# Statistics of seven early layernorms split between VectorE and GpSimd, and a new planned order of all engines, in a four-layer graph network

## The chip, the cores and the metric

The kernel runs on one core of a Trainium2 chip. The metric is the device time of one execution in microseconds (us). A core has five engines with a queue each: TensorE (PE in the profile; its weight loads are PEld), VectorE (DVE), ScalarE (ACT), GpSimd (POOL) and SyncE (SP), which here only starts transfers (DMAs).

## The reference

x is 32 graphs of 512 nodes with 128 features, adj a 512 x 512 matrix of zeros and ones. Each of the four layers adds a network of a layernorm to x:

```python
def _layernorm(x, axis=-1, eps=1e-5):
    m = jnp.mean(x, axis=axis, keepdims=True)
    v = jnp.var(x, axis=axis, keepdims=True)
    return (x - m) / jnp.sqrt(v + eps)

h = jnp.maximum(_layernorm(x, axis=-1), 0.0)
x = x + _L0_gnn_ref(h, adj, ...)   # edge scores: sigmoid(a_tgt + a_src), times a mask of adj; two ELUs
h = jnp.maximum(_layernorm(x, axis=-1), 0.0)
x = x + _L1_gnn_ref(h, adj, adj, ...)   # five gated steps with adj @ h: gates z and r, candidate tanh
h = jnp.maximum(_layernorm(x, axis=-1), 0.0)
x = x + _L2_gnn_ref(h, adj, ...)   # adj @ (h @ weight) + bias
h = jnp.maximum(_layernorm(x, axis=-1), 0.0)
x = x + _L3_gnn_ref(h, adj, adj, ...)   # h, adj @ h, adj^2 @ h, adj^3 @ h, each times a weight, summed
```

## The kernel before, in words

The program first describes its work to a planner and then issues it in the order that the planner finds. Each `op(engine, us, due, emit, reads, writes, ...)` is one step: an engine, an assumed duration, a due time, a function that issues its instructions, and the values that it reads and writes. `Plan.order` plays the engines through with those assumed times: on each engine the ready step with the earliest due time goes first, and buffers are given out as they come free. The result is a fixed order for every engine; on the chip each engine works its own queue strictly in that order and waits by semaphores. `Plan.nudge` draws random shifts of due times, one draw for each seed in `HEAD_NUDGES` (steps due from 0 to 130) and `TAIL_NUDGES` (steps due after 1430; empty before), so a seed more or less changes the order everywhere after it. `plan.idle` (L375) is a product of ones on TensorE that the planner puts in, in the first 50 us, where TensorE would have nothing to do.

`A_LANDS` holds for each of the four quarters of the adjacency when the planner takes it to have landed after its DMA was issued; two are loaded from SyncE's queue, two from ScalarE's. `adjacency_turned` (L608) transposes the quarters on TensorE. VectorE counts the entries that are not zero or one (L594, summed on TensorE at L623), and the program then branches: the arm for a binary adjacency is the one that runs. In it the adjacency's square is made at L974 (products in fp32r, one pass), and the masks on GpSimd (L892).

A graph is 512 rows of 128 in four blocks of 128 rows (`NC` = 4). The graphs go through the layers staggered, up to five groups of four in flight. `layernorm` (L544) has these steps: on VectorE the statistics of each block (`bn_stats`, L553, four instructions: count, mean and squared deviations of the even and of the odd elements), their joining to mean and variance (`bn_aggr`, L555, four), and one addition of epsilon (L556); on GpSimd the power -1/2 (L558); then either, with ReLU, the shift on VectorE (L562) and four scalings on ScalarE (L567), or, for graphs 0 to 3 in layer 0, four normalisations on VectorE (L573), where the ReLU comes after a transpose. `entry` makes the layernorm of layer 0, `layer1`'s is made in the loop at the end of `list_rest`.

Layer 0: `scored` makes the first ELU (exponential, tanh and ReLU on ScalarE; L641, L646 and L648 on VectorE), the messages and scores (L711, L718), and `aggregated` the masked edge scores (L757 on ScalarE, L760 on VectorE), their products (L769), row sums (`totals`, on GpSimd's and SyncE's queues, L680 and L802), a second ELU and the output products (L830), which are added to x at L541. Layer 1: products with the adjacency in fp32r (L1018), with the gates' weights in fp32 (L521, two passes each), gates on VectorE and ScalarE (L1043 to L1064, L526), and transposes by blocks through DRAM (L462 on VectorE, then a DMA `m<-f` and one `f<-m`). Layer 3 has products with folded weights (L1093), with the squared adjacency (L1106), the last addition (L1125) and the stores.

Of the kernel before, what the change touches and what calls it, by code (L numbers as in the profile page):

```python
# [15 lines left out]
ALU = mybir.AluOpType  # L16
# [3 lines left out]
EPS = 1e-5  # L20
STEPS = 5


HEAD, TAIL = 250.0, 1430.0
HEAD_NUDGES = (7100008, 7100429, 7300015, 7100544, 7100583, 7300139, 7300091, 7300684, 7300016, 7300033, 7300035,
    7300041, 7300077, 7300137, 7300140, 7300167, 7300172, 7300174, 7300178, 7300506, 7300199,
    7300249, 7300263, 7300279, 7300298, 7300305, 7300507, 14000074, 14000497, 7300344, 7300346,
    7300367, 7300389, 7300391, 7300393, 7300406, 7300423, 14000795, 7300482, 7300509, 7300510,
    7300530, 7300532, 7300539, 7300544, 14000157, 7300549, 7300551, 7300553, 7300562, 7300570,
    14000024, 14000577, 7300614, 7300629, 7300644, 14000027, 14000360, 7300654, 7300663, 7300681,  # L30
    14000347, 7300696, 14000026, 14000010, 14000014, 14000195, 14000023, 14000035, 14000039,
    14000042, 14000045, 14000046, 14000048, 14000088, 14000208, 14000563, 14000122, 14000125,
    14000164, 14000166, 14000167, 14000181, 14000182, 14000252, 14000186, 14000187, 14000189,
    14000198, 14000204, 14000210, 14000212, 14000213, 14000739, 14000219, 14000227, 14000231,
    14000243, 14000275, 14000289, 14000299, 14000304, 14000306, 14000385, 14000319, 14000324,
    14000325, 14000326, 14000333, 14000338, 14000345, 14000346, 14000355, 14000358, 14000364,
    14000665, 14000398, 14000472, 14000417, 14000426, 14000427, 14000432, 14000438, 14000440,
    14000451, 14000458, 14000463, 14000469, 14000485, 14000486, 14000515, 14000520, 14000521,
    14000647, 14000528, 14000531, 14000540, 14000596, 14000560, 14000561, 14000815, 14000569,
    14000570, 14000580, 14000589, 14000591, 14000597, 14000602, 14000605, 14000606, 14000609,  # L40
    14000629, 14000638, 14000654, 14000661, 14000689, 14000678, 14000681, 14000685, 14000686,
    14000697, 14000698, 14000700, 14000703, 14000708, 14000715, 14000716, 14000721, 14000723,
    14000725, 14000726, 14000732, 14000734, 14000744, 14000751, 14000753, 14000755, 14000788,
    14000796, 14000801, 14000804, 14000807, 14000808, 14000811, 14000816, 14000817, 14000818,
    14000822, 14000827, 14000829, 14000831, 14000836, 14000839, 14000842, 14000843, 14000847,
    14000849, 14000850, 14000851, 14000852, 14000853, 14000855, 14000856, 14000857, 14000860,
    14000864, 14000870, 14000871)
TAIL_NUDGES = ()


class Val:
# [222 lines left out]
def tile_four_graph_layers(  # L274
# [27 lines left out]
    nc = tc.nc  # L302
    B, N, D = x.shape
    NC = N // P
    G = 4
# [4 lines left out]
    PACE, FIRST_PACE, LAST_PACE = 56.0, 10.0, 30.0  # L310
    BRANCH, FILL = 9.0, 50.0
    MARGIN = 10.0
    FIRST = 4
    FIRST_TREE, TREES, TREE = 4, 30, 52
    ONES, COPIES = 0, 32
    HALF = 2
    SQUARE, NAT = 11.0, 3.0
    BRANCHES = 0.75
    A_LANDS = (3.87, 3.05, 4.2, 4.0)

    T_MM, T_TR, T_NARROW, T_PASS = 0.86, 0.44, 0.224, 0.23
    T_VEC, T_COPY, T_ACT, T_DMA = 0.605, 0.5, 0.6, 0.45
# [3 lines left out]
    op = plan.op  # L326
# [22 lines left out]
    def at(v):  # L349
        if v.tile is not None:  # L350
            return v.tile
        return places[v.kind][v.slot] if v.whole is None else at(v.whole)[:, v.part]
# [15 lines left out]
    ident, ones, neg_half = const("ident", [P, P]), const("ones", [P, P]), const("nhalf", [P, NC])  # L368
# [31 lines left out]
    X = [Val(whole=X_group[b // G], part=b % G) for b in range(B)]  # L400
# [11 lines left out]
    A_nat = [Val("f") for _ in range(NC)]  # L412
# [128 lines left out]
            nc.vector.tensor_tensor(xv, xv, t, op=ALU.add)  # L541
        op("DVE", T_VEC, due, add, [X[b], p], [X[b]], two=two)

    def layernorm(b, due, relu=True, earliest=0.0):  # L544

        s, h = Val("s"), Val("f")
        def stat(lo, k=1):
            t = at(s)[:, lo * NC : (lo + k) * NC]
            return t if k == 1 else t.rearrange("p (c k) -> p c k", k=k)
        VAR, SCALE, SHIFT, PAIRS, STATS = 0, 1, 2, 4, 6  # L550
        def moments():
            for c in range(NC):
                nc.vector.bn_stats(stat(STATS, 6)[:, c, :], at(X[b])[:, c, :])  # L553
            for c in range(NC):
                nc.vector.bn_aggr(stat(PAIRS, 2)[:, c, :], stat(STATS, 6)[:, c, :])  # L555
            nc.vector.tensor_scalar(stat(VAR), stat(PAIRS, 2)[:, :, 1], EPS, None, op0=ALU.add)  # L556
        op("DVE", 1.26, due, moments, [X[b]], [s], earliest=earliest)
        op("POOL", 1.2, due, lambda: nc.gpsimd.tensor_tensor(  # L558
            stat(SCALE), stat(VAR), at(neg_half), op=ALU.pow), [s, neg_half], [s], two=False)
        mean = lambda: stat(PAIRS, 2)[:, :, 0]  # L560
        if relu:
            op("DVE", 0.1, due, lambda: nc.vector.scalar_tensor_tensor(  # L562
                stat(SHIFT), mean(), -1.0, stat(SCALE), op0=ALU.mult, op1=ALU.mult),
                [s], [s], two=True)
        def scale():
            for c in range(NC):
                nc.scalar.activation(  # L567
                    at(h)[:, ts(c, P)], at(X[b])[:, c, :], AF.Relu,
                    bias=stat(SHIFT)[:, c : c + 1], scale=stat(SCALE)[:, c : c + 1],
                )  # L570
        def normed():
            for c in range(NC):
                nc.vector.tensor_scalar(  # L573
                    at(h)[:, ts(c, P)], at(X[b])[:, c, :], mean()[:, c : c + 1],
                    stat(SCALE)[:, c : c + 1], op0=ALU.subtract, op1=ALU.mult)
        if relu:
            op("ACT", 1.56, due, scale, [X[b], s], [h])
        else:
            op("DVE", 1.03, due, normed, [X[b], s], [h])
        return h  # L580
# [11 lines left out]
    for ic in range(NC):  # L592
        odd = Val("f")
        op("DVE", 0.62, -1, lambda ic=ic, odd=odd: nc.vector.scalar_tensor_tensor(  # L594
            at(odd), at(A_nat[ic]), 0.0, at(A_nat[ic]),
            op0=ALU.is_gt, op1=ALU.not_equal, accum_out=at(n_odd[ic])),
            [A_nat[ic]], [odd, n_odd[ic]], two=True)
    def by_token(v):
        return at(v).rearrange("p (t c) -> p c t", c=NC)

    def adjacency_turned(due):
        banks = [Val("b") for _ in range(NC)]
        for pt in banks:
            pt.pieces = True
        for ic in range(NC):
            def turn(ic=ic):
                for jc, pt in enumerate(banks):
                    nc.tensor.transpose(at(pt)[:, ts(ic, P)], by_token(A_nat[ic])[:, jc, :], at(ident))  # L608
            op("PE", T_TR, due + ic, turn, [A_nat[ic], ident], banks)
        return banks  # L610

    adj_r = rows_of(const("adj_r", [P, NC, N], F32R).tile)
# [225 lines left out]
    def begin(b):  # L838
        steady = min(b, B - G - 1)
        return max((steady - G) * PACE + (b - steady) * LAST_PACE, b * FIRST_PACE)  # L840

    def entry(b):
        h = layernorm(b, begin(b), relu=b >= FIRST, earliest=begin(b) - 12.0 if b < G else 0.0)
        return first_turned(b, h, begin(b)) if b < G else turned_back(h, begin(b))

    begun = [scored(b, entry(b), begin(b)) for b in range(G)]
# [14 lines left out]
    def arm(binary):  # L861
        with ExitStack() as stack:
# [11 lines left out]
            if not binary:  # L874
                issue(plan.order())
                return
            plan.nudge(0.0, 130.0, HEAD_NUDGES)
            order = [*plan.order(end=HEAD), *plan.order(end=TAIL)]
            plan.nudge(TAIL, 2000.0, TAIL_NUDGES)
            issue(order + plan.order())  # L880

    def list_rest(binary, pool):
# [70 lines left out]
        for half in range(2):  # L953
            t, outs = Val("f"), slice(half * P // 2, (half + 1) * P // 2)
# [206 lines left out]
        for g in range(NG):  # L1161
            bs = range(g * G, (g + 1) * G)
            hT, uT = [], []
            for b in bs:
                if g:
                    load_graph(b, max(begin(b) - 40, 4 + b))
                    aggregated(b, scored(b, entry(b), begin(b)), begin(b), halves)
                t = begin(b) + (0.75 if b < G else 2.2 if b < B - G - 1 else 1.2) * PACE
                layer1(b, layernorm(b, t), t + 6, G * PACE / STEPS)
                t += (G + 0.5) * PACE  # L1170
                layer2(b, layernorm(b, t), t + 6)
                t += 0.5 * PACE
                h = layernorm(b, t)
                if g < NG - 1:
                    hT.append(turned_back(h, t + 4, in_order=True))
                else:
                    hT.append(copied(transposed(h, t + 6), t + 6))
                if binary:
                    uT.append(copied(times_adj(parts(h, t + 4, two=True), t + 6), t + 6))

            layer3(g, hT, uT, t + 12, {NG - 2: 16.0, NG - 1: 8.0}.get(g, 14.0))
            X_group[g].left -= 1
# [46 lines left out]
```

## Time and profile before

| what | before |
|---|---|
| median of 3 runs (range) | 1594.95 us (1594.51 to 1596.13) |
| profiled execution | 1594.3 us |
| its span | 1592.4 us |
| mean granted TensorE clock | 0.999 |
| busy VectorE, ScalarE, GpSimd | 1414.9, 1135.6, 303.8 us |
| `bn_aggr` (L555), 512 instructions | 46.6 us busy |
| addition of epsilon (L556), 128 instructions | 22.0 us busy |
| power on GpSimd (L558), 128 instructions | 156.0 us busy |

The times are those of the profiled execution from its span's start. "Busy" sums an engine's instructions. A group line gives line, engine, operation, output and input, shape and count, then busy us and mean ns, then the idle time of the engine ahead of it with what ended it. The chain of work that ended last is followed back from the last instruction, at each step to what released it, and is shown in order of time: start, us, what. A two-pass fp32 product stands as two records.

### The profile page before, as it was taken

What the parts mean: (1) busy time and instruction counts of PE and PEld (TensorE: products, weight loads), DVE (VectorE), ACT (ScalarE), POOL (GpSimd) and SP (SyncE); (2) the same over time, 40 slices, a digit from 0 to 9 for tenths busy, and PEclk for the clock granted to TensorE, in tenths of its full rate; (3) what the DMA queues carried; (4) which work ended last, traced back from release to release, by engine and by line L of the source; (5) the groups of instructions that cost most, each with busy time, mean ns of one, the idle gap of its engine ahead of it and who ended that gap; (6) DMA issues with size and microseconds to landing.
All of it is one profiled execution on the core that took longest, in us unless ns stands there. A gap on an engine that the chain in (4) does not pass through costs nothing.

```text
span 1592.4 us, 21245 instructions
## 1 busy us (share of the span) xinstructions
PE 1586.2 (100%) x6279; PEld 1017.0 (64%) x6279; DVE 1414.9 (89%) x3367; ACT 1135.6 (71%) x2151; POOL 303.8 (19%) x297
## 2 busy tenths in 40 slices
PE   9999999999999999999999999999999999999998
PEld 7655555666666666666666666666666666656688
DVE  8999999999988999898999989989899898988772
ACT  7877776877776777677876777667687676755661
POOL 3322112212211212211222121221221111000010
PEclk9999999999999999999999999999999999999999
DMA  4465545564554556554555545555556554322221
GB/s 129 94 164 145 157 120 133 127 170 120 138 144 122 141 145 146 132 139 126 147 146 142 143 116 148 128 139 137 139 152 151 129 140 125 96 86 87 93 54 56
DMA packets 303062, 204.92 MB, mean 129 GB/s; under 512 B 94936, under 2 KB 245080, under 8 KB 302936
## 3 DMA queue, kind: packets, MB, share of 16 engines
q1 hardware_dynamic: 260808, 175.63, 36.0%
q0 software_dynamic: 39984, 26.38, 13.1%
q10 hardware_dynamic: 2144, 1.44, 0.3%
q8 instruction: 52, 0.85, 0.2%
q14 instruction: 74, 0.61, 0.1%
HBM read 96.41 MB, written 103.68 MB: 126 GB/s over the span
## 4 chain that ended last, share of the span: by engine, by line
PE 95%; DVE 2%; DMA 2%; ACT 0%; issue 0%; SPq 0%; DVEq 0%
PE b L521 43%; PE b L1018 26%; PE b L1093 7%; PE b L769 6%; PE b L1106 4%; PE b L830 3%; PE b L1081 2%; PE b L711 2%; PE b L821 2%; DMA f<-m 0%; DVE f L760 0%; DMA m<-f 0%; DMA f<-in_adj_dram 0%; DMA f<-d 0%; DVE f L648 0%; DVE f L646 0%
## 5 line engine op out<-in xcount | busy, mean ns | idle before, releaser
L510 ACT COPY f<-b 128x512 f32<-128x512 f32 x414 | 238.5, 585 | 179.2 <-PE b L1018 121.5
L558 POOL TENSOR_TENSOR s<-s,nhalf 128x4 f32<-128x4 f32 x128 | 156.0, 1221 | 768.8 <-DVE s L556 745.6
L1043 DVE TENSOR_TENSOR f<-f,b 128x512 f32<-128x512 f32 x320 | 213.5, 680 | 49.6 <-PE b L521 43.3
L1018 PE MATMUL b<-AQ,r 128*128 128x512 f32 x848 | 256.4, 432 | 0.0
L567 ACT ACTIVATE f<-x,s 128x128 f32<-128x128 f32 x496 | 204.2, 488 | 20.7 <-DVE s L562 18.4
L462 DVE STREAM_TRANSPOSE f<-f 128x512 f32<-128x512 f32 x246 | 206.5, 846 | 7.6 <-ACT f L567 6.3
L1018 PEld LDWEIGHTS b<-AQ,r 128*128 128x128 f32 x848 | 158.9, 188 | 69.5 <-issue 31.4
L1018 PE MATMUL b<-adj_r,r 128*128 128x512 f32 x640 | 193.7, 428 | 0.0
L526 ACT ACTIVATE f<-f,b4w 128x512 f32<-128x512 f32 x160 | 115.3, 721 | 96.4 <-DVE f L1043 95.6
L521 PE MATMUL b<-f,w4T 128*128 128x512 f32 x320 | 163.2, 593 | 0.1
L521 PE MATMUL b<-f,u5T 128*128 128x512 f32 x320 | 163.1, 593 | 0.0
L521 PE MATMUL b<-f,w5T 128*128 128x512 f32 x320 | 162.9, 592 | 0.0
L521 PE MATMUL b<-f,w3T 128*128 128x512 f32 x320 | 162.8, 592 | 0.0
L521 PE MATMUL b<-f,u3T 128*128 128x512 f32 x320 | 161.7, 592 | 0.0
L1018 PEld LDWEIGHTS b<-adj_r,r 128*128 128x128 f32 x640 | 120.0, 188 | 50.0 <-issue 21.3
L526 ACT ACTIVATE f<-b,b5w 128x512 f32<-128x512 f32 x160 | 109.5, 686 | 50.3 <-PE b L521 49.5
L526 ACT ACTIVATE f<-f,b3w 128x512 f32<-128x512 f32 x160 | 114.8, 719 | 35.7 <-DVE f L1043 35.0
L680 POOL DMA_DIRECT2D m<-f x78 | 71.0, 910 | 333.1 <-DVE f L1060 45.3
L1093 PEld LDWEIGHTS b<-V,f 128*128 128x128 f32 x1024 | 122.2, 192 | 16.0 <-issue 13.9
L1060 DVE TENSOR_TENSOR f<-f,f 128x512 f32<-128x512 f32 x160 | 109.2, 683 | 24.3 <-ACT f L526 23.6
L988 ACT CAST r<-f 128x512 fp32r<-128x512 f32 x197 | 120.5, 617 | 12.6 <-DMA f<-m 9.6
L992 DVE TENSOR_TENSOR r<-f,r 128x512 fp32r<-128x512 f32 x168 | 113.9, 682 | 12.9 <-ACT r L988 12.8
(138 smaller groups left out, 2665.9 us busy)
## 6 DMA issues: line engine op xcount, KB each, us to landing
m<-f SPq DMA_DIRECT2D x272, 256.0 KB
f<-m SPq DMA_DIRECT2D x186, 256.0 KB
m<-f POOLq DMA_DIRECT2D x78, 256.0 KB, 4.2
f<-m SPq DMA_DIRECT2D x240, 64.0 KB
f<-d SPq DMA_DIRECT2D x54, 256.0 KB
x<-in_x_dram SPq DMA_DIRECT2D x32, 256.0 KB
out_dram<-x SPq DMA_DIRECT2D x28, 256.0 KB
d<-y SPq DMA_DIRECT2D x54, 64.0 KB
```

What stands on the lines that cost most here:

```text
L462: op("DVE", us, due, lambda: nc.vector.transpose(view_out(at(blocks)), view_in(at(src))), [src], [blocks])
L510: op("ACT", us, due, lambda: nc.scalar.copy(at(t), at(src)), [src], [t])
L521: nc.tensor.matmul(to, at(w), of, start=start, stop=stop)
L526: op("ACT", us, due, lambda: nc.scalar.activation(at(dst), at(src), AF.Tanh, bias=at(bias), scale=scale), [src, bias], [dst])
L558: op("POOL", 1.2, due, lambda: nc.gpsimd.tensor_tensor(stat(SCALE), stat(VAR), at(neg_half), op=ALU.pow), [s, neg_half], [s], two=False)
L567: nc.scalar.activation(at(h)[:, ts(c, P)], at(X[b])[:, c, :], AF.Relu, bias=stat(SHIFT)[:, c : c + 1], scale=stat(SCALE)[:, c : c + 1],)
L988: op("ACT", T_COPY, due, lambda: nc.scalar.copy(part(hi), whole()), [src], [hi], keep=1)
L992: op("DVE", T_VEC, due, lambda: nc.vector.tensor_tensor(part(lo), whole(), part(hi).bitcast(F32), op=ALU.subtract), [src, hi], [lo], two=two)
L1018: nc.tensor.matmul(at(pa), at(part)[:, ts(jc, P)], view(at(columns[jc])), start=jc == n == 0, stop=jc == NC - 1 and n == PARTS - 1,)
L1043: op("DVE", T_VEC, d, lambda: nc.vector.tensor_tensor(at(s), at(u), at(pg), op=ALU.add), [u, pg], [s])
L1060: op("DVE", T_VEC, d, lambda c=c, h=h: nc.vector.tensor_tensor(at(c), at(c), at(h), op=ALU.subtract), [c, h], [c], two=True)
L1093: nc.tensor.matmul(at(pz)[:, ts(i, D)], at(t[i])[:, ts(ic, P)], at(V[k]), start=i == graphs[0] and n == 0, stop=last and i == graphs[-1] a ...
```

## The change

1. `layernorm` gets a second form, `by_pool`, for graphs 1, 2, 3 in layer 0 and 0 to 3 in layer 1. VectorE makes only the `bn_stats`; GpSimd joins the halves itself with eight small instructions on 128 x 4 elements, and then takes the power as before.
2. `A_LANDS` has other assumed landings, and the transpose of an adjacency quarter is taken as 0.48 us instead of 0.44. Both are numbers for the planner alone.
3. `HEAD_NUDGES` is another, longer list of seeds, of which some are those of before, and `TAIL_NUDGES` has 24 seeds.

The second and third issue nothing themselves, but the order of every engine comes out of them.

```diff
-HEAD_NUDGES = (7100008, 7100429, 7300015, 7100544, 7100583, 7300139, 7300091, 7300684, 7300016, 7300033, 7300035,
...
-TAIL_NUDGES = ()
+HEAD_NUDGES = (7100008, 7100429, 7300139, 7300016, 7300033, 7300041, 7300137, 7300140, 7300167, 7300174, 7300178,
...
+TAIL_NUDGES = (40500041, 40500004, 40500007, 40500043, 40500032, 40500075, 40500021, 40500022, 40500023, 40500082,
...
+    POOL_0, POOL_1, POOLED = (1, 2, 3), (0, 1, 2, 3), 1.7
...
-    A_LANDS = (3.87, 3.05, 4.2, 4.0)
+    A_LANDS = (4.2, 3.05, 4.7, 4.28)
...
-    def layernorm(b, due, relu=True, earliest=0.0):
+    def layernorm(b, due, relu=True, earliest=0.0, by_pool=False):
...
+        if by_pool:
+            MEAN, T, U = 4, 5, 3
+            even, odd = (lambda k: stat(STATS, 6)[:, :, k]), (lambda k: stat(STATS, 6)[:, :, 3 + k])
+            def stats():
+                for c in range(NC):
+                    nc.vector.bn_stats(stat(STATS, 6)[:, c, :], at(X[b])[:, c, :])
+            op("DVE", 0.9, due, stats, [X[b]], [s], earliest=earliest)
+            def moments():
+                tt, ts1 = nc.gpsimd.tensor_tensor, nc.gpsimd.tensor_scalar
+                tt(stat(T), even(1), odd(1), op=ALU.subtract)
+                tt(stat(U), even(2), odd(2), op=ALU.add)
+                tt(stat(T), stat(T), stat(T), op=ALU.mult)
+                ts1(stat(T), stat(T), D / 4.0, None, op0=ALU.mult)
+                tt(stat(VAR), stat(T), stat(U), op=ALU.add)
+                ts1(stat(VAR), stat(VAR), 1.0 / D, EPS, op0=ALU.mult, op1=ALU.add)
+                tt(stat(MEAN), even(1), odd(1), op=ALU.add)
+                ts1(stat(MEAN), stat(MEAN), 0.5, None, op0=ALU.mult)
+                tt(stat(SCALE), stat(VAR), at(neg_half), op=ALU.pow)
+            op("POOL", 1.2 + POOLED, due, moments, [s, neg_half], [s], two=False)
+            mean = lambda: stat(MEAN)
+        else:
...
-            op("PE", T_TR, due + ic, turn, [A_nat[ic], ident], banks)
+            op("PE", 0.48, due + ic, turn, [A_nat[ic], ident], banks)
...
-        h = layernorm(b, begin(b), relu=b >= FIRST, earliest=begin(b) - 12.0 if b < G else 0.0)
+        h = layernorm(b, begin(b), relu=b >= FIRST, by_pool=b in POOL_0, earliest=begin(b) - 12.0 if b < G else 0.0)
...
-                layer1(b, layernorm(b, t), t + 6, G * PACE / STEPS)
+                layer1(b, layernorm(b, t, by_pool=b in POOL_1), t + 6, G * PACE / STEPS)
```

## The prediction

> **What bounds the kernel now.** I read four views in this order: the page's busy times, the groups of TensorE instructions by shape, the chain that ended last, and the waits of TensorE. The first:
>
> ```profile
> PE 1586.2 (100%) x6279; PEld 1017.0 (64%) x6279; DVE 1414.9 (89%) x3367; ACT 1135.6 (71%) x2151; POOL 303.8 (19%) x297
> ```
>
> A busy TensorE (PE) at 100% proves nothing by itself, since ends of matmuls are modelled. So I count the work by issue intervals. The chain gives them, where it stays on TensorE:
>
> ```profile
> 163.37 8.58 PE b L521 x20
> ...
> 279.91 3.71 PE b L1018 x16
> ...
> 1566.00 8.93 PE b L1093 x80
> ```
>
> That is 0.429 us for one record of a two-pass fp32 product 512 wide (8.58/20), 0.232 for an fp32r one 512 wide, 0.1116 for one 128 wide. The groups by shape give the counts, of which the largest and the idle products are:
>
> ```profile
> L1018 PE MATMUL b<-AQ,r 128*128 128x512 f32 x848 | 256.4, 432 | 0.0
> L521 PE MATMUL b<-f,w4T 128*128 128x512 f32 x320 | 163.2, 593 | 0.1
> L1093 PE MATMUL b<-V,f 128*128 128x128 f32 x1024 | 123.5, 275 | 0.0
> L375 PE MATMUL b<-ones 128*128 128x128 f32 x70 | 11.8, 320 | 1.0 <-DVE ones L370 1.0
> ```
>
> All groups together: 1992 records of fp32 512 wide (L521 1672, L769 256, L821 64) at 0.429 are 854.6 us; 2068 of fp32r 512 wide (L1018 1792, L1106 248, three small groups 28) at 0.232 are 479.8; 2125 of 128 wide without the idle ones at 0.1116 are 237.2; the rest 2.2. Sum: 1573.8 us. The first transpose starts at 6.13 us, the last matmul ends its issue at 1588.0: 1581.9 us. So only 8.1 us after the adjacency's arrival is not needed work. Of that, 50 of the 70 records of L375 (products of ones that the order puts in while TensorE has nothing) are 5.6, and true idle time about 2.5. Ahead stand 6.1 us (loads), behind 4.4 us (the last addition and its store). The whole profiled execution is 1594.3 us, 1.9 above its span and 0.65 below the median of 1594.95.
>
> So whatever the new order does, it can win at most 8.1 us (0.5%). The change takes no product of the computation away; it moves them.
>
> The chain shows where the little slack is made:
>
> ```profile
> 20.35 0.29 DVE s L555 x4
> 20.64 0.02 issue
> 20.66 0.17 DVE s L556
> ...
> 51.39 1.16 PE b L711 x8
> ```
>
> From 19.2 to 51.4 us it lies on VectorE (DVE), which is busy 39.8 of the 40 us from 20 to 60, and 0.48 us of it is L555 and L556 of each layernorm. After 51.4 it is on TensorE with short breaks.
>
> **The change part by part.** *The statistics.* Seven layernorms (graphs 1 to 3 in layer 0, 0 to 3 in layer 1) lose L555 and L556 on VectorE: 7 x 0.48 = 3.4 us off VectorE, about half of it inside the stretch where VectorE is the chain. GpSimd (POOL) gets eight small instructions more for each. Their nearest rows, and that of the power, which stays:
>
> ```profile
> 20.91 1.01 POOL L558 TENSOR_TENSOR s<-s,nhalf 128x4 f32<-128x4 f32 x1 [2.24 <-DVE s L556]
> ...
> 22.09 0.18 POOL L936 TENSOR_TENSOR b5w<-b5w,b5u 128x1 f32<-128x1 f32 x1
> 22.24 0.22 POOL L939 TENSOR_SCALAR b3w<-b3w 128x1 f32<-128x1 f32 x1
> ...
> 67.41 0.54 POOL L960 COPY V<-f 128x64 f32<-128x64 f32 x1
> ...
> 72.83 3.29 POOL L960 COPY V<-f 128x64 f32<-128x64 f32 x1
> ```
>
> Start to start the small ones are 0.2 us, so the chain is 8 x 0.2 + 1.0 = 2.6 us, against 1.0 now. The Trainium skill speaks against it: its page GPSIMD Engine Reference, Specifications, says that GpSimd's SBUF interfaces are shared with VectorE and contended by VectorE instructions with two SBUF inputs. L960 above agrees: 0.54 us once, 3.29 beside two-input instructions of VectorE (L1050, L760). If each small instruction had to let one of them (0.68 us) pass, the chain would be 8 x 0.88 + 1.4 = 8.4 us. But the power itself, on operands of the same 128x4, has a median of 1.32 and a maximum of 1.99 over 128 uses, most of them beside a busy VectorE: a stretch of 1.3. I take 2.6 x 1.3 = 3.4 us and keep 2.6 to 8.4. The planner allows 2.9.
>
> Who waits: on VectorE the shift (L562) or, in layer 0, the normalisation L573, and everything behind it. In the new order graph 1's L573 follows just one other statistics instruction, so VectorE will stand still there: its statistics end at about 10.9 us, the bias scaling and 2.6 to 3.4 us follow on GpSimd, so L573 begins near 14.0 to 14.7 and not at 13.2 as now. Behind it is graph 0's ELU (L646), which now starts at 15.1; L573 takes 1.1 us, so it is 0 to 0.7 us late. TensorE has all 16 products of the adjacency's square ahead of it in the new order, and idle products after them, so I charge 0 to 0.5 us. The masks (L892, 0.62 us each) come behind the chain, at about 14 to 17 instead of 10.8 to 14.8; they are first read at 23.3, so they are covered by 6 us, and would cost their own lateness without.
>
> *What VectorE's relief gives.* At the rows' durations, VectorE's work ahead of the first addition to x (L541) falls from 42.1 to 37.7 us in the new order, TensorE's up to the output products before it from 43.1 to 41.4; at the sixth addition it is 149.8 to 141.3 and 145.5 to 141.5. So VectorE is less behind than now, by some 3 to 4 us. But TensorE has little to gain from it: the order holds 32 idle products of ones instead of 35 (two records each). One more stands before the adjacency, where TensorE waits anyway until 6.13; 21 instead of 25 stand after it: 4 x 0.22 = 0.9 us. Two of these are in the wait for the count of odd entries, which VectorE sets, so they turn into idle time: 0.4 us remains sure, 0.9 at best.
>
> *Waits.* The trace's own:
>
> ```profile
> PE b L608 <- DMA f<-in_adj_dram: 0.5, 1, 0.5
> PE b L830 <- DVE f L648: 0.2, 1, 0.2
> ```
>
> By the starts of TensorE's instructions in the timeline, gaps of over 0.05 us after 8 us sum to 2.5 us, 2.0 of them before 150 us (the larger at 20.0, 51.4, 73.6, 125.2). With VectorE less behind, a third of the early ones should go (-0.7); the new order brings its own, as any order does whose times were assumed beforehand (+0.5, as much as the present one shows after 150).
>
> *The landings (A_LANDS), the transposes' 0.48, the nudges.* These are numbers for the planner alone and cost nothing themselves. The adjacency's transposes stand in the same order as now and wait for the same load; SyncE's first loads are the same twelve. TAIL_NUDGES move work after about 1430 us, where the gaps are a few hundredths of a us each, and the last products and stores are the same: 0. All other orders change too, with no work added.
>
> Sum: -0.6 - 0.7 + 0.5 + 0.2 = -0.6 us on the profiled 1594.3, so 1593.7, and with the 0.65 us to the median 1594.3.
>
> By another rule the sum would differ. The Trainium skill (Perfetto Trace Analysis, Identifying the Most-Contended Engine) calls matmul busy time a bad measure and takes weight loads' busy share instead. That is 64% here, which would leave 36% of the span free and make VectorE (89%) the engine to relieve; its 3.4 us would then show in full, 1591.5. The issue intervals above leave 8.1 us, so here the weight loads mislead, and I keep -0.6.
>
> **The rivals.** *A: VectorE's relief counts in full* and the order uses it: -3.4 us or more, 1588 to 1591.7. For it: the chain on VectorE from 19 to 51 us. Against: TensorE is idle or on idle products for only about 4 us there, and the new order still holds 15 idle products behind the branch (now 17). Chance 0.06.
>
> *B: GpSimd's chain is near its upper bound.* If it is over about 4 us, VectorE waits at the seven L562 and L573 for some 1 us each, at a time when it has no slack, and TensorE behind it: +4 us, 1598 to 1600, slower. For it: 3.29 us of L960. Against: the stretch of 1.3 of the power. Chance 0.07.
>
> *C: the new order meets a transfer later than assumed.* The blocks turned through DRAM land 3 to 7 us after their issue (6.60 us for one m<-f at 553, which ends in the gap at 568.5). Several such gaps of 0.5 to 2 us would give +2 to +6, 1596.5 to 1600. Against: after 150 us the present order loses 0.5 us in all. Chance 0.15, with 0.09 of it over the bound.
>
> The forecast (0.72) covers 1592.5 to 1597. That the change does nothing to the time lies in it.
>
> **How the numbers follow.** A measurement tells about 0.2% (3.2 us), so 1591.8 to 1598.1, from no change. Faster: A, 0.06. Slower: 0.07 + 0.09 = 0.16. Same: 0.78. The range from 1592.3 to 1598.0 leaves out A and the slower parts of B and C, about 0.2.
>
> **What would show it.** Right: some 64 records of L375's successor, gaps of TensorE of 2 to 3 us in sum, a VectorE chain that ends before 50 us, GpSimd's nine instructions in 2.6 to 3.7 us, and the same 4.4 us at the end. Wrong: idle gaps of TensorE of over 4 us in sum, each to be named by its releaser (GpSimd for B, a DMA for C), or a span under 1589 (A).

## The result and the profile after

The changed kernel takes 1600.12 us (median of 9 runs, 1599.11 to 1601.79) against 1594.95 before (also 9 runs): a ratio of 1.0033 with a 95% interval of 1.0025 to 1.0042, so 5.2 us slower. The profiled execution has a span of 1599.0 us, 6.6 more than before. The page's busy times after:

```profile
PE 1588.5 (99%) x6273; PEld 1016.4 (64%) x6273; DVE 1411.5 (88%) x3332; ACT 1140.0 (71%) x2151; POOL 324.7 (20%) x353
```

VectorE has 3.4 us less, as summed; GpSimd has 20.9 more. TensorE's work is the same, so the time must be in its gaps. Its waits after, the longest four of the change's stretch (who waited for whom: us, times, longest):

```profile
PE b L774 <- DVE f L711: 1.3, 1, 1.3
PE b L832 <- DVE f L823: 1.1, 1, 1.1
...
PE b L893 <- DVE f L711: 0.9, 1, 0.9
PE b L563 <- DMA f<-m: 0.5, 1, 0.5
```

(Line numbers of the changed kernel are 42 to 63 higher: L711 is L648 of before, L774 L711, L823 L760, L832 L769, L893 L830, L563 L521, L625 L562, L636 L573. L602 to L609 are the eight new instructions on GpSimd, L610 is the power.) The first gap's origin is seen in the timeline of GpSimd and VectorE (start, us, engine, line):

```profile
47.26 0.68 DVE L709 SCALAR_TENSOR_TENSOR f<-f,f 128x512 f32<-128x512 f32 x1
47.42 1.78 POOL L602 TENSOR_TENSOR s<-s 128x4 f32<-128x4 f32 x1 [16.66 <-DVE s L598]
47.85 0.68 DVE L858 TENSOR_TENSOR f<-f,f 128x512 f32<-128x512 f32 x1
48.45 0.69 DVE L711 SCALAR_TENSOR_TENSOR f<-f,f 128x512 f32<-128x512 f32 x1
49.06 0.22 DVE L781 TENSOR_SCALAR s<-b,be_quarter 128x4 f32<-128x4 f32 x1
49.16 1.98 POOL L603 TENSOR_TENSOR s<-s 128x4 f32<-128x4 f32 x1
49.19 0.68 DVE L858 TENSOR_TENSOR f<-f,f 128x512 f32<-128x512 f32 x1
49.79 0.69 DVE L709 SCALAR_TENSOR_TENSOR f<-f,f 128x512 f32<-128x512 f32 x1
50.39 0.68 DVE L858 TENSOR_TENSOR f<-f,f 128x512 f32<-128x512 f32 x1
51.09 0.19 POOL L604 TENSOR_TENSOR s<-s 128x4 f32<-128x4 f32 x1
...
52.62 1.05 POOL L610 TENSOR_TENSOR s<-s,nhalf 128x4 f32<-128x4 f32 x1
53.70 0.16 DVE L625 SCALAR_TENSOR_TENSOR s<-s 128x4 f32<-128x4 f32 x1 [2.63 <-POOL s L610]
53.78 0.68 DVE L711 SCALAR_TENSOR_TENSOR f<-f,f 128x512 f32<-128x512 f32 x1
```

L602 and L603 are instructions on 128 x 4 elements that take 0.2 us elsewhere. Here each ends only when a row of VectorE's instructions with two SBUF inputs ends: 47.26 to 49.14, then 49.19 to 51.07. Between the rows stands L781, which reads PSUM, and one small instruction gets through. Then VectorE comes to L625, which needs the chain, and stands still for 2.63 us; behind it waits L711, and behind that TensorE's L774, which starts at 54.61 after a gap of 1.3 to 1.5 us. The seven chains from L602 to the power's end take 2.90, 3.55, 5.24, 6.24, 5.30, 5.05 and 3.37 us (4.5 on average) where the planner had 2.9. VectorE's waits for the power, in the shift and in the normalisation:

```profile
DVE s L625 <- POOL s L610: 4.8, 4, 2.6
DVE f L636 <- POOL s L610: 4.4, 2, 2.9
```

The first of these six waits (2.94 us) stands behind the first chain, which ran without a hold in 2.90: it is the chain's length alone. The other five (1.42, 2.63, 1.57, 0.40 and 0.21 us) are each shorter than what their chain took over 2.90 (2.34, 3.34, 2.40, 2.15 and 0.47 us). By the timeline these chains would have been done in time without the holds. No kernel with the same eight instructions unheld was run, so this division into length and hold is read from the trace and not measured by itself.

### The profile page after: what moved, and what is told of

Same layout as the page of the kernel before. It is cut to its first block, busy times and chain, and to the rows that moved or that the text cites. A ratio compares the mean times of both kernels' runs of the same rounds, so it can differ in the third digit from the quotient of the medians.

```text
span 1599.0 us, 21231 instructions
## 1 busy us (share of the span) xinstructions
PE 1588.5 (99%) x6273; PEld 1016.4 (64%) x6273; DVE 1411.5 (88%) x3332; ACT 1140.0 (71%) x2151; POOL 324.7 (20%) x353
## 4 chain that ended last, share of the span: by engine, by line
PE 95%; POOL 2%; DVE 1%; DMA 1%; issue 1%; ACT 0%; SPq 0%; POOLq 0%
PE b L563 44%; PE b L1081 26%; PE b L1156 7%; PE b L832 6%; PE b L1169 4%; PE b L893 3%; PE b L1144 2%; PE b L884 2%; PE b L774 1%; DVE f L823 0%; DMA f<-d 0%; POOL s L610 0%; DMA d<-y 0%; DMA f<-in_adj_dram 0%; DMA bi_sb<-in_L_gnn_bi_dram 0%
## 5 line engine op out<-in xcount | busy, mean ns | idle before, releaser
L621 POOL TENSOR_TENSOR s<-s,nhalf 128x4 f32<-128x4 f32 x121 | 148.7, 1229 | 723.8 <-DVE s L619 656.5
L1081 PE MATMUL b<-AQ,r 128*128 128x512 f32 x856 | 260.5, 434 | 0.0
L1081 PE MATMUL b<-adj_r,r 128*128 128x512 f32 x616 | 188.5, 428 | 0.0
L563 PE MATMUL b<-f,w3T 128*128 128x512 f32 x320 | 162.9, 592 | 0.0
L563 PE MATMUL b<-f,w4T 128*128 128x512 f32 x320 | 162.9, 592 | 0.0
L563 PE MATMUL b<-f,w5T 128*128 128x512 f32 x320 | 162.6, 592 | 0.0
L563 PE MATMUL b<-f,u5T 128*128 128x512 f32 x320 | 162.4, 592 | 0.0
L563 PE MATMUL b<-f,u3T 128*128 128x512 f32 x320 | 161.4, 592 | 0.5 <-DMA f<-m 0.5
L1081 PEld LDWEIGHTS b<-adj_r,r 128*128 128x128 f32 x616 | 115.1, 188 | 45.9 <-issue 17.9
L1156 PE MATMUL b<-V,f 128*128 128x128 f32 x1024 | 123.7, 275 | 0.0
```

Of the source, the lines that this page charges most:

```text
L563: nc.tensor.matmul(to, at(w), of, start=start, stop=stop)
L621: op("POOL", 1.2, due, lambda: nc.gpsimd.tensor_tensor(stat(SCALE), stat(VAR), at(neg_half), op=ALU.pow), [s, neg_half], [s], two=False)
L1081: nc.tensor.matmul(at(pa), at(part)[:, ts(jc, P)], view(at(columns[jc])), start=jc == n == 0, stop=jc == NC - 1 and n == PARTS - 1,)
L1156: nc.tensor.matmul(at(pz)[:, ts(i, D)], at(t[i])[:, ts(ic, P)], at(V[k]), start=i == graphs[0] and n == 0, stop=last and i == graphs[-1] a ...
```

## The experiments

Two theories stood at the start. Theory 1: GpSimd's chain is held up and keeps VectorE's queue, and TensorE, waiting. Theory 2: the new order itself meets late inputs, above all transfers. All kernels but the last two keep the planned durations, so that the order of every engine stays exactly that of the kernel named, and change only what the seven layernorms issue. Each ratio is against the kernel before as it was timed in the same session (medians of 1594.62 to 1595.22 us), so a difference between two runs is that between what each is above its own median of before.

**The join back on VectorE, in the new order**

```diff
             def stats():
...
+                for c in range(NC):
+                    nc.vector.bn_aggr(stat(PAIRS, 2)[:, c, :], stat(STATS, 6)[:, c, :])
+                nc.vector.tensor_scalar(stat(VAR), stat(PAIRS, 2)[:, :, 1], EPS, None, op0=ALU.add)
             op("DVE", 0.9, due, stats, [X[b]], [s], earliest=earliest)
             def moments():
...
-                tt(stat(T), even(1), odd(1), op=ALU.subtract)
...
-                ts1(stat(MEAN), stat(MEAN), 0.5, None, op0=ALU.mult)
                 tt(stat(SCALE), stat(VAR), at(neg_half), op=ALU.pow)
...
```

> The order of every engine as in the changed kernel, but the seven layernorms join their statistics on VectorE again (bn_aggr and the addition of epsilon), so that GpSimd has the power alone. Theory 1 (GpSimd's chain, held up beside VectorE's two-input instructions, keeps VectorE's queue waiting at 51 to 54 and 61 to 65 us, and with it TensorE): the gaps at 54.6, 55.7 and 66.2 (3.1 us) go, those at 114.7 and 123.9 (1.8 us) stay; VectorE has 3.4 us more to do, of which 1 to 2 come back; 1596.5 to 1598.5. Theory 2 (the new order itself meets late transfers and late inputs): 1600 to 1602, as the changed kernel or worse by VectorE's work.

Measured: 1597.22 us, ratio 1.0013 (1.0005 to 1.0021). That is inside theory 1's band: some 2.8 us of the loss go, 2.4 stay. The gaps from 50 to 100 us, where theory 1 saw them go, only fall from 4.1 to 2.5 us (table below), presumably since VectorE now has the work itself.

**No join at all, in the new order**

```diff
-                tt(stat(T), even(1), odd(1), op=ALU.subtract)
...
-                tt(stat(SCALE), stat(VAR), at(neg_half), op=ALU.pow)
+                tt(stat(SCALE), even(2), at(neg_half), op=ALU.pow)
...
-            mean = lambda: stat(MEAN)
+            mean = lambda: even(1)
```

> The order as in the changed kernel, the join of the statistics left out on both engines: the power is taken of the even half's squared deviations, the mean is that of the even half, so the computation lacks the odd half. Theory 1: the gaps between 15 and 70 us fall from 6 us to under 2; 1595 to 1596.5, and what is left above the kernel before is the gaps at 114.7 and 123.9. Theory 2: 1599 to 1600.

Measured: 1593.46 us, ratio 0.9993 (0.9985 to 1.0001). Faster than theory 1 had it, since the gaps near 115 and 124 us are gone too. The order is the same, so they followed from the early delay and not from transfers that are late by themselves. Its waits of TensorE, complete (L417 is L375 of before, L984 L929, L663 L608):

```profile
PE b L417 <- DVE ones L412: 1.0, 1, 1.0
PE b L984 <- DMA f<-in_L_gnn_u_w_dram: 0.7, 1, 0.7
PE b L663 <- DMA f<-in_adj_dram: 0.5, 1, 0.5
```

Nothing is left but the start and one weight's load. That load, 0.7 us, is all that theory 2 can point to here. It doesn't explain the changed kernel, whose trace has no wait for it; but this kernel's chains are also some 1.6 us shorter than the planner had them, which could hide a small lateness elsewhere.

**GpSimd's join in the old order**

```diff
...
-        op("DVE", 1.26, due, moments, [X[b]], [s], earliest=earliest)
...
+            op("DVE", 1.26, due, stats, [X[b]], [s], earliest=earliest)
+            def moments():
+                tt, ts1 = nc.gpsimd.tensor_tensor, nc.gpsimd.tensor_scalar
+                tt(stat(T), even(1), odd(1), op=ALU.subtract)
...
+            op("POOL", 1.2, due, moments, [s, neg_half], [s], two=False)
```

> The order of every engine as in the kernel before, but in the seven layernorms GpSimd joins the statistics with the eight small instructions. Theory 1: the chain takes 3 to 6 us each time where the order allows 1.2, VectorE waits for it and TensorE behind it: 1598 to 1603. Theory 2: the chain is hidden or paid for by VectorE's 3.4 us less: 1594 to 1596.

Measured: 1608.47 us, ratio 1.0083 (1.0069 to 1.0096), over the top of theory 1's band. Its chains take 2.9 to 4.5 us (3.8 on average) where this order allows 1.2.

**No join in the old order** (the same edit as above with the old order)

> The order as in the kernel before, the join of the statistics left out on both engines in the seven layernorms (the odd half is missing from mean and variance). It prices what VectorE's 3.4 us are worth at best in the old order. By the count of TensorE's work only the gaps of about 1 us that VectorE makes can go: 1593.5 to 1595. If VectorE's chain from 19 to 51 us counted in full, it would be 1591.5 to 1593.

Measured: 1595.51 us, ratio 1.0004 (0.9996 to 1.0012): no gain from 3.4 us less on VectorE. It is just above the first band, and far from the second. Where its gaps from 100 to 150 us come from (2.7 us in the table) was not followed up.

The gaps of TensorE, counted by its issue intervals as in the prediction, add up to this (us):

```
kernel                        10-50  50-100  100-150   10-150   span
before                          0.8     0.8      0.6      2.2   1592.4
after                           3.3     4.1      2.7     10.0   1599.0
join on VectorE, new order      2.4     2.5      2.2      7.1   1595.9
no join, new order              1.5     0.2      0.1      1.8   1591.2
join on GpSimd, old order       5.7     6.0      3.8     15.5   1605.8
no join, old order              1.4     0.2      2.7      4.2   1594.0
```

After 150 us every kernel has 3.6 to 4.2 us, which is mostly jitter of 0.01 us a piece. The changed kernel has 7.8 us more of gaps than the one before and 0.7 to 0.9 us less of idle products, together about 7.0 us. Its span grew by 6.6 us; the remaining 0.4 us are no more than the kernels differ after 150 us.

What holds GpSimd was then tested. Theory 1a: only its two-input instructions are held. Theory 1b: all are.

**One input only, new order**

```diff
-                tt(stat(T), even(1), odd(1), op=ALU.subtract)
-                tt(stat(U), even(2), odd(2), op=ALU.add)
...
+                ts1(stat(T), even(1), 1.0, None, op0=ALU.mult)
+                ts1(stat(U), even(2), 2.0, None, op0=ALU.mult)
...
```

> The order as in the changed kernel, GpSimd still has eight small instructions on the same operands in each of the seven layernorms, but each has one tensor input and a number (tensor_scalar), so the odd half is missing from the statistics. Theory 1a (a two-input instruction of GpSimd is held while VectorE runs its two-input instructions[...]): without second inputs the chains are near 2.9 us as the planner has them, with only the power still held at times, and the time is 1593.5 to 1596. Theory 1b (GpSimd's small instructions are held beside VectorE whatever their inputs, or eight of them are just too long): chains of 4 to 6 us stay and the time is 1598 to 1601.

Measured: 1601.29 us, ratio 1.0036 (1.0022 to 1.0049), 0.3 us above 1b's band. Its seven chains take 4.5 us on average, as with two inputs. Theory 1a falls. Three lines of its timeline say it. The first stands beside a row of four instructions of VectorE; L602 and L603, which have one input now, stand beside the same rows as those of 1.78 and 1.98 us above:

```profile
23.17 2.47 POOL L607 TENSOR_SCALAR s<-s 128x4 f32<-128x4 f32 x1
...
48.09 1.80 POOL L602 TENSOR_SCALAR s<-s 128x4 f32<-128x4 f32 x1 [16.68 <-DVE s L598]
49.86 1.96 POOL L603 TENSOR_SCALAR s<-s 128x4 f32<-128x4 f32 x1
```

**One input only, old order** (the same edit)

> The same one-input instructions in the order of the kernel before, where GpSimd's chain was planned at 1.2 us. It splits the 13.6 us that the join on GpSimd costs in this order into length and hold. Theory 1a: chains of 2.9 instead of 3.8 on average; the length alone is 1.7 us over the plan for each of seven, part of it hidden: 1598 to 1604. Theory 1b: chains as before, 1607 to 1609.

Measured: 1610.03 us, ratio 1.0091 (1.0075 to 1.0106), a little above 1b's band; chains of 3.0 to 4.6 us. 1a falls here too.

**Which layernorms**: GpSimd's join in layer 0 alone, then in layer 1 alone, in the new order (`if not relu` is layer 0 alone, `if relu` in its place layer 1 alone; in the other layer VectorE joins)

```diff
...
+                if not relu:
+                    tt(stat(T), even(1), odd(1), op=ALU.subtract)
...
```

> The order as in the changed kernel; GpSimd joins the statistics in layer 0 (graphs 1 to 3), VectorE again in layer 1 (graphs 0 to 3). The chains on GpSimd that ran 5 to 6 us beside gaps at 54.6 and 66.2 are those of layer 1. Theory 1: these gaps shrink to those of the join on VectorE, the gaps of 15 to 35 us stay as in the changed kernel: 1596.5 to 1598.5. If instead the early delay of layer 0's chains is what all later gaps come from: 1599 to 1600.5.

Measured: 1597.08 us, ratio 1.0013 (1.0004 to 1.0021), inside theory 1's band.

> The counterpart of the one with layer 0 alone (1597.08): the order as in the changed kernel, layer 0's three joins on VectorE, layer 1's four on GpSimd. If layer 1's long holds (6.2, 5.3, 5.1 us) carry the loss, about 1599 to 1601, as with all seven; if the loss comes from both alike, 1597 to 1598.5.

Measured: 1599.63 us, ratio 1.0035 (1.0021 to 1.0049). That is the band in which layer 1's holds carry the loss. Layer 0's three joins cost the same on either engine (1597.08 us with them on GpSimd, 1597.22 with them on VectorE). Layer 1's four, with chains of 6.25, 5.30, 5.05 and 3.37 us, bring a further 2.6 us (against the join on VectorE) to 3.3 us (all seven against layer 0 alone). One thing disturbs this run: TensorE waits in its trace for the load that the kernel without a join had waited 0.7 us for, and longer:

```profile
PE b L997 <- DMA f<-in_L_gnn_u_w_dram: 1.7, 1, 1.7
PE b L779 <- DVE f L716: 1.3, 1, 1.3
```

(L997 is L929 of before, L779 L711, L716 L648.) So part of its time can be this load. The gaps that layer 1's chains make are still plain: L779's 1.3 us is that of L774 above, at 54.6 us in the changed kernel, and the kernel with layer 0 alone has no such wait.

**The planner told the measured duration**

```diff
-    POOL_0, POOL_1, POOLED = (1, 2, 3), (0, 1, 2, 3), 1.7
+    POOL_0, POOL_1, POOLED = (1, 2, 3), (0, 1, 2, 3), 3.3
```

> The changed kernel with one number of the planner corrected: GpSimd's join is taken as 3.3 us instead of 1.7, so that the chain counts 4.5 us, the mean of the seven in the trace. The order is made anew with the same seeds. Theory 1 with a well planned wait: TensorE's gaps become planned idle products; the order holds 51 of them after the adjacency instead of 21 (6.7 us more), against 7 us of gaps that go: 1598 to 1603. If the wrong duration alone were to blame, and the plan could hide the chain once it knew it: 1593 to 1596.

Measured: 1617.65 us, ratio 1.0144 (1.0128 to 1.0159), worse than both had it. A reason that fits, but wasn't tested, is that the seeds suit one set of durations: 124 records of idle products stand in its trace (64 in the changed kernel's), and gaps of 2 to 3 us more in each of the stretches 100 to 130, 130 to 150 and 150 to 200. It doesn't tell whether a plan searched anew with this duration could hide the chain; that wasn't tried.

**The hold by itself**: nothing of the reference is computed; in each of eight stretches GpSimd runs one small instruction that starts with VectorE's row (L85), eight more (L67, or L69 with one input) and a power (L88), beside sixteen instructions of VectorE of one kind back to back (64 short ones for bn_stats). It was run once. The stretches in order:

```python
plan = [(None, two_in), (both, two_in), (both, one_in), (with_psum, two_in),
        (one, two_in), (turn, two_in), (stats, two_in), (None, one_in)]
```

> None of the reference's computation: only the disputed cost, and zeros stored. Eight stretches; in each GpSimd runs nine small instructions on 128 x 4 and a power, beside sixteen instructions of VectorE 512 wide, back to back: nothing; two SBUF inputs; two SBUF inputs with GpSimd's small ones having one input; one SBUF and one PSUM input; one SBUF input (tensor_scalar); the 32 x 32 transpose; bn_stats; nothing, with one-input small ones. Theory 1c (GpSimd is held as long as VectorE runs instructions with two SBUF inputs back to back, whatever GpSimd's own inputs): GpSimd's chain takes about 3 us alone, with PSUM, transpose and bn_stats, and about 10 to 13 us in the two stretches with two SBUF inputs, of which one small instruction alone shows 8 to 10. Rival (any busy VectorE slows each small instruction): chains of 4 to 6 us in every stretch with VectorE busy, no single one over 1.5. The stretch with tensor_scalar is open between the two.

GpSimd's timeline: alone, beside two SBUF inputs (four lines, of two stretches), one PSUM input, tensor_scalar, transpose and bn_stats; then VectorE's row behind the 9.61:

```profile
2.85 2.14 POOL L67 TENSOR_TENSOR work<-work 128x4 f32<-128x4 f32 x8
...
7.01 4.74 POOL L67 TENSOR_TENSOR work<-work 128x4 f32<-128x4 f32 x8
11.83 1.34 POOL L88 TENSOR_TENSOR mark<-work,nhalf 128x4 f32<-128x4 f32 x1
...
16.07 9.61 POOL L85 TENSOR_TENSOR work<-mark 128x4 f32<-128x4 f32 x1 [2.90 <-DVE mark L89]
25.76 2.36 POOL L69 TENSOR_SCALAR work<-work 128x4 f32<-128x4 f32 x8
...
29.80 2.14 POOL L67 TENSOR_TENSOR work<-work 128x4 f32<-128x4 f32 x8
...
39.54 2.61 POOL L67 TENSOR_TENSOR work<-work 128x4 f32<-128x4 f32 x8
...
44.87 2.14 POOL L67 TENSOR_TENSOR work<-work 128x4 f32<-128x4 f32 x8
...
54.44 2.14 POOL L67 TENSOR_TENSOR work<-work 128x4 f32<-128x4 f32 x8
```

```profile
15.90 9.71 DVE L55 SCALAR_TENSOR_TENSOR C<-A,Bt 128x512 f32<-128x512 f32 x16
```

Theory 1c holds for one of the two stretches with two SBUF inputs: there one small instruction takes 9.61 us, the whole row. With PSUM, transpose and bn_stats the eight take 2.14 us, as alone. In the other stretch it fails: the eight take 4.74 us and start 0.60 us apart, just as VectorE's do, so one is let through with each of VectorE's. That is 0.33 us more for each, and the power behind them takes 0.33 more as well (1.34 against 1.01). Beside tensor_scalar, 2.61 us, they keep step with VectorE too, 0.33 to 0.34 us apart both; that row's instructions are just shorter.

Two things this kernel doesn't show. The one-input instructions (25.76) came when the row had ended at 25.61, since the two-input L85 ahead of them was the one that was held: that one input makes no difference rests on the two runs above. And what decides between the two forms is open: in both stretches L85 started 0.17 us behind the row's first instruction. Both forms stand in the changed kernel's trace (the lines from 47 to 51 us, and 0.5 to 0.7 us a piece from 61 to 64 us).

## Why the prediction was wrong

- **TensorE's bound** was right. All spans above follow from the same 1573.8 us of work, the gaps and the idle products; the best of them (no join, new order) won 1.4 of the 8.1 us.
- **VectorE's relief** was sized rightly: 3.4 us off its busy time. "TensorE has little to gain from it" is what the kernels without a join show: 1.4 us less than before in the new order, none in the old. What I missed is that the new order needs that relief: with the join on VectorE it is 3.8 us slower than with none, where in the old order leaving the join out gains nothing. Without a join the sum's other terms came about as written: 0.7 to 0.9 us less of idle products (-0.6) and 0.4 less of gaps (-0.7 + 0.5).
- **The failed step** is "I take 2.6 x 1.3 = 3.4 us and keep 2.6 to 8.4" for GpSimd's chain, and with it the +0.2 us that the sum has for its lateness. The chain measured 4.5 us on average and over 5 in four of seven. The 1.3 came from the power, one instruction of 1.0 us that had mostly 0.3 more. I made a factor of what is an addition: in the kernel with the hold alone a small instruction of 0.27 us had the same 0.33 more as the power of 1.01, and eight small ones give eight occasions for it. A whole row's hold comes on top. The 3.29 us of L960 showed one already: it ran beside five instructions of VectorE in a row (72.80 to 75.97 us), where my estimate let each small one wait for a single one. Seven unheld chains of 2.90 are 20.3 us, the measured ones 31.7: 11.4 us of holds that the order doesn't contain.
- **The charge for waiting** named graph 1's normalisation alone. The other six layernorms stand in the sum at nothing, with no reason given, though rival B says of them that VectorE has no slack there. VectorE's five waits behind held chains come to 6.2 us; the four joins of layer 1 are what costs more on GpSimd than on VectorE, and the three of layer 0, with graph 1's among them, cost the same. Against no join, 6.5 us reached the end (5.2 slower than before instead of 1.4 faster).
- **Who waits** was right in kind: VectorE at the shift, the ELU behind it, TensorE behind that. Rival B's price for a chain "over about 4 us", which was "+4 us, 1598 to 1600, slower", is near what came (+5.2); I gave it a chance of 0.07, and the range ended at 1598.0.
- **Graph 1's normalisation** began at 14.2 us, within the 14.0 to 14.7; but it took 2.08 us instead of 1.1, beside GpSimd's masks. The 1.1 was misread: it is that of groups with no mask beside them. The group that stood in this place before took 1.73, of which the two instructions beside a mask took 0.66 and 0.64 us each, the others 0.34 and 0.33. The ELU behind it began at 16.2, not at 15.1. The masks themselves, ready by 17.4, were covered until 23.3, as said. The normalisations before; then after, beside masks and beside small instructions of GpSimd alone:

```profile
13.16 1.73 DVE L573 TENSOR_SCALAR f<-x,s 128x128 f32<-128x128 f32 x4
```

```profile
14.19 2.08 DVE L636 TENSOR_SCALAR f<-x,s 128x128 f32<-128x128 f32 x4 [2.94 <-POOL s L610]
...
26.63 1.11 DVE L636 TENSOR_SCALAR f<-x,s 128x128 f32<-128x128 f32 x4 [1.42 <-POOL s L610]
```

- **Rival C** had the gaps at 115 and 124 us on its side in the changed kernel's own trace, one of them released by a DMA. Without the join they are not there: a wait on a transfer need not be the transfer's fault. The wait on a transfer that stays without the join is that for a weight's load near 19 us: 0.7 us without a join, 0.8 with the join on VectorE, 1.7 with GpSimd's join in layer 1 alone, and no wait on it in the changed kernel's trace. So it varies from run to run and doesn't explain the changed kernel's loss.
- **The rule of weight loads' share** (the Trainium skill, Perfetto Trace Analysis, Identifying the Most-Contended Engine) was rightly set aside: the share is 64% in both kernels, before and after 5 us were lost. (The page names the share of peak arithmetic beside it, which the prediction didn't work out.) The rule on shared SBUF interfaces (GPSIMD Engine Reference, Specifications), which I priced but did not follow, was the one that decided. It names two SBUF inputs, as measured. Its other case is a mode with two ports; the tensor_scalar stretch cost 0.5 us in eight, but no run shows whether it was in that mode.

## What to carry to other kernels

Before a small step is moved to GpSimd, look at what VectorE runs at that time. Beside rows of instructions with two SBUF inputs each small instruction may last as long as the row; beside PSUM inputs, transposes and bn_stats it took no longer than alone. Price such a chain by its worst row in the trace, not by a factor on a longer instruction, and ask what is queued behind the instruction of VectorE that waits for it. This order, planned to a hundredth of a microsecond, had no slack for durations that were wrong by 2 to 3 us, and the relief of VectorE that it had already spent couldn't be given back without loss: 3.8 us with the join on VectorE again.

## What the runs showed of the hardware

- GpSimd's own inputs made no difference: instructions on 128 x 4 were held 1.80 and 1.96 us with one input where they had been held 1.78 and 1.98 with two.
- A row of sixteen two-input instructions (9.71 us) held one small instruction of GpSimd for 9.61 us; another such row let one through each 0.60 us. Beside PSUM inputs, transposes and bn_stats eight took 2.14 us, as alone.
- VectorE is slowed the other way too: a normalisation of 128 x 128 took 0.64 to 0.67 us beside a mask on 128 x 512 of GpSimd's, and 0.34 beside a power on 128 x 4.
